# Degrees and gates of a four-layer graph network as products in four column groups of TensorE

## The chip, the cores and the metric

The kernel runs on one core of one Trainium2 chip. A core has TensorE (PE; its weight loads are PEld), VectorE (DVE), ScalarE (ACT), GpSimd (POOL) and SyncE (SP), each with an instruction stream of its own. They meet at semaphores and share the on-chip SBUF and the accumulators in PSUM. The metric is the time of one execution on the device, in microseconds (us), as a median over runs: less is better.

## The reference

Sixteen graphs ("batches") of 1024 nodes with 128 features pass through four layers; each layer is added to its input and layer-normed. The adjacency is 1024 x 1024, of zeros and ones, symmetric. Cut to what matters:

```python
# layer 0: attention with one gate
h = x @ W.T + b;  e = (h @ A) @ h.T;  e = e + e.T
att = softmax(where(adj > 0, e, -9e15), axis=1) * adj
hp = relu(att @ h);  c = sigmoid(concat[x, hp] @ gate_w.T + gate_b)
x = LN(x + c * x + (1 - c) * hp)

# layer 1: thinned adjacency, then three SAGE steps
adj_d = dilate(adj)                       # row after row
def sage(x, Wr, Wx, b):
    deg = clip(sum(adj_d, -1), 1, None)   # the degrees
    out = (adj_d @ x) / deg @ Wr + x @ Wx + b
    return out / norm(out) * mask
# h1, h2, h3: sage, relu and batch norm over all batches, one after the other
x = LN(x + (concat[h1, h2, h3] * mask @ Wl + bl) * mask)

# layer 2: attention with three gates
h, e, att, hp as in layer 0 (masked entries are 0 ahead of the softmax)
i, f, o = [sigmoid(concat[x, hp] @ g_w.T + g_b) for g in ("ig", "fg", "og")]
x = LN(x + o * tanh(sigmoid(i * hp + f * x)))

# layer 3: graph convolution, A = D^-1/2 (adj + I) D^-1/2
h = elu(elu(x @ W0 + b0));  h = elu(A @ (h @ W1) + b1)
x = LN(x + A @ (h @ W2) + b2)
```

## The kernel before

All work of the profile lies in the fast path (from line 640 on). A general fallback behind a run-time flag is compiled in as well and isn't run. A batch's 1024 nodes lie as 8 row tiles (NT) of 128 (P); wide results go in two halves (H2) of 512 columns, a PSUM bank each. Layers 0 and 2 keep features on the partitions for products ("xT", "hT", "hpT", 128 x 1024) and nodes on the partitions for the norms ("xn", "yn").

Stage 1 (lines 882 to 995) does layer 0 batch by batch; the dilation follows (1005 to 1181). Layer 1 (1237 to 1471) goes three times over the batches, as each batch norm needs all of them: first batches 8 to 15, whose thinned adjacency is still in SBUF ("carry", fp8), then 0 to 7, whose adjacency is loaded again ("A8"). In the first of the three steps a batch passes four generators, which take turns: `load`, `first` (of the next batch), `out` (of this one) and `keep` (of the one before). `first` has the degrees (1352 to 1363): `degree_product` multiplies a constant weight of 128 equal columns ("twos", over the tensor "step") with the adjacency, so that every PSUM partition gets the row of the column sums; ACT copies partition 0 as "row" (1357), a DMA turns it to 8 x 128 ("d16"), DVE takes a minimum over it (1360), clips and inverts it (1362, 1363), and a DMA writes it to memory, from where it is read back as "rdeg" on all partitions. Then come the transposes of x, the split of x in "hi" and "lo" (1251 on ACT, 1252 on DVE), the widening of the adjacency to four-byte pieces "a" (1271, 1273) and the product of both (1284), scaled by "rdeg" (1376). `out` multiplies with the two weights (1388), and has the row norms: "o" on DVE (1390), squares on ACT (1396), "ss" on DVE (1397). `keep` transposes the result and makes the product with the adjacency for the next step.

Layers 2 and 3 (1477 to 1660) are one pipeline over the batches. `in_turn` (807) interleaves `after` of batch b-1, `attention` of batch b and `before` of batch b+1. `attention` (1563) runs over 8 row tiles: mask on ACT (1571), scores on PE ("pmm", 723), masked maximum on DVE (1576), exponential on ACT (1580), sums on DVE, and the product with h on PE (1590), accumulated over the tiles in one PSUM tile "acc". `after` (1593) takes the ReLU of it ("hpT", 1596), forms the three gates ("pg", 1600 and 1601), adds the bias (1603), takes the sigmoid through tanh on ACT (1604), combines (1608 to 1614, with the transposes of hpT at 758), norms (741 on DVE, 744 on POOL, 796 on DVE, 798 on ACT) and then does layer 3: A widened to four bytes (1626 on ACT, 1639 on DVE), the transposes, the product with U0 (765), two elus (1498 to 1504), the product with U1 (1513), the propagation (1527), and both again with U2. `before` (1532) applies layer 1's last linear map (765, 1539) and norm, and prepares xT, hT, G and hn.

The order of instructions on each engine isn't the program's order: a scheduler sets it when the kernel is built, from the instructions and what they depend on, so that an edit can move others too. The tiles come from pools with a fixed number of buffers; layer 1's products have four PSUM banks "acc" and four "ph", layers 2 and 3 have two banks "ph".

Layer 0's gate has a helper, `gates` (768 to 780), that the edit uses again. It multiplies a narrow weight (32 columns) with a quarter of the 1024 nodes in each of four column groups of the PE array, side by side, and turns the result to have the nodes on partitions:

```python
for q in range(4):
    nc.tensor.matmul(p[32 * q:32 * q + 32, :], g, x[:, q * N // 4:(q + 1) * N // 4], start=(i == 0),
                     stop=(i == len(pairs) - 1), tile_position=(0, 32 * q))
...
nc.scalar.copy(out, p)
p = psum.tile([P, 2, P], F32, name="pg", tag="h")
for t in range(2):
    nc.tensor.transpose(p[:, t, :], out[:, t * P:(t + 1) * P], identf)
return p.rearrange("p t (q g) -> p q t g", q=4)
```

Of the kernel before, what the change touches and what calls it, by code (L numbers as in the profile page):

```python
# [9 lines left out]
F32 = mybir.dt.float32  # L10
# [12 lines left out]
P = 128  # L23
# [616 lines left out]
def fast_kernel(ctx: ExitStack, tc: tile.TileContext, t: dict, out: bass.AP, flag: bass.AP):  # L640

    nc = tc.nc
    B, N, D = t["x"].shape
    NT = N // P
    H2 = N // 512
# [122 lines left out]
    def gates(psum, out, *pairs):  # L768


        p = psum.tile([P, N // 4], F32, name="pq", tag="h")
        for i, (g, x) in enumerate(pairs):
# [8 lines that stand above are left out]
# [82 lines left out]
    twos = step[:, P:]  # L863
# [18 lines left out]
    with ExitStack() as ph:  # L882

        early = ph.enter_context(tc.tile_pool(name="l0_early", bufs=1, reuse_waits="tile"))
        wts = ph.enter_context(tc.tile_pool(name="l0_w", bufs=1, reuse_waits="tile"))
# [10 lines left out]
        gw = wts.tile([P, 2, 32], F32, name="l0gw")  # L896
# [286 lines left out]
    class Layers23:  # L1183
# [8 lines left out]
        def weights(self, ps_h):  # L1192
            wts = self.wts
            self.Wl = wts.tile([P, 3, P], F32, name="Wl")
            nc.sync.dma_start(self.Wl, nat(t["L1_gnn_Wl"]))
            self.blcol = column(wts, t["L1_gnn_bl"], "blcol")
            self.W2T = transposed(wts, ps_h, matrix(wts, t["L2_gnn_W_w"], "l2W"), "l2WT", "h")
            self.b2 = column(wts, t["L2_gnn_W_b"], "l2b")
            self.As2 = symmetric(wts, ps_h, matrix(wts, t["L2_gnn_A"], "l2A"), "l2As", "h")
            self.gw = wts.tile([P, 2, 3], F32, name="l2gw")  # L1200
            self.gb = wts.tile([P, 3], F32, name="l2gb")
            for i, n in enumerate(("ig", "fg", "og")):
                with nc.allow_non_contiguous_dma(reason="a vector of 256"):
                    nc.sync.dma_start(self.gw[:, :, i], t[f"L2_gnn_{n}_w"].rearrange("o (h d) -> d (o h)", d=P))
                src = t[f"L2_gnn_{n}_b"]
                nc.sync.dma_start(self.gb[:, i:i + 1], bass.AP(tensor=src.tensor, offset=src.offset, ap=[[0, P], [1, 1]]))
            self.U = [matrix(wts, t[f"L3_gnn_W{i}"], f"U{i}") for i in range(3)]
            self.c = [column(wts, t[f"L3_gnn_b{i}"], f"c{i}") for i in range(3)]
            self.nbig = wts.tile([P, 1], F32, name="nbig")
            nc.vector.memset(self.nbig, -BIG)  # L1210
# [26 lines left out]
    with ExitStack() as ph:  # L1237
# [16 lines left out]

        def degree_product(A):

            for h in range(H2):
                c = slice(h * 512, (h + 1) * 512)
                acc = ps_a.tile([P, 512], F32, name="acc")
                for jt in range(NT):  # L1260
                    nc.tensor.matmul(acc, twos[:, :P], A[:, jt, c], start=(jt == 0), stop=(jt == NT - 1))
                yield acc, c

        def widened(A):

# [22 lines left out]
        class Step:  # L1288
# [63 lines left out]
            def first(self, b):  # L1352

                st = self.batches[b]
                row = work.tile([1, N], F16, name="row", bufs=1)
                for acc, c in degree_product(st.A):
                    nc.scalar.copy(row[:, c], acc[0:1, :])
                d16 = small.tile([NT, P], F16, name="d16", bufs=1)
                nc.gpsimd.dma_start(d16, row)
                nc.vector.tensor_reduce(nodeg[:NT, b:b + 1], d16, AX.X, OP.min)  # L1360
                d8 = small.tile([NT, P], F32, name="d8", bufs=1)
                nc.vector.tensor_scalar(d8, d16, 0.5, 1.0, op0=OP.mult, op1=OP.max)
                nc.vector.reciprocal(d8, d8)
                nc.gpsimd.dma_start(rdeg_d[b], d8)
                self.load_rdeg(b)
                yield
                st.hT = work.tile([P, N], F32, name="hT")
                for p, c, _ in turned(ps_h, st.x):
                    nc.scalar.copy(st.hT[:, c], p)
                yield  # L1370
                parts = split(st.x)
                pieces = list(widened(st.A))
                yield
                st.ag = work.tile([P, N], F32, name="ag", bufs=3)
                for acc, c in adjacency_product(pieces, parts):
                    nc.vector.tensor_mul(st.ag[:, c], acc, st.rdeg[:, c])
                    yield
# [99 lines left out]
    with ExitStack() as ph:  # L1477
# [10 lines left out]
        def wide(name, bufs=1, dtype=F32):  # L1488
            return work.tile([P, N], dtype, name=name, bufs=bufs)
# [103 lines left out]
        def after(s, b):  # L1593

            hpT = wide("hpT")
            nc.scalar.activation(hpT, s.acc, AF.Relu)
            pg = ps_h.tile([P, NT, 3], F32, name="pg", tag="h")
            for i in range(NT):
                c = slice(i * P, (i + 1) * P)
                nc.tensor.matmul(pg[:, i, :], s.xT[:, c], gw[:, 0, :], start=True, stop=False)  # L1600
                nc.tensor.matmul(pg[:, i, :], hpT[:, c], gw[:, 1, :], start=False, stop=True)
            gt = small.tile([P, NT, 3], F32, name="gt")
            nc.vector.tensor_add(gt, pg, gb[:, None, :].to_broadcast([P, NT, 3]))
            nc.scalar.activation(gt, gt, AF.Tanh, scale=0.5)
            nc.vector.tensor_scalar(gt, gt, 0.5, 0.5, op0=OP.mult, op1=OP.add)
            yn = rows("yn", 2)
            for p, c, k in turned(ps_h, hpT):
                nc.vector.tensor_mul(yn[:, k, :], tiles3(p), half_rows(gt[:, k, 0]))
            f = rows("x3T")
            nc.vector.tensor_mul(f, s.xn, per_row(gt[:, :, 1]))  # L1610
            nc.vector.tensor_add(yn, yn, f)
            nc.scalar.activation(yn, yn, AF.Tanh, scale=0.5)
            nc.scalar.activation(yn, yn, AF.Tanh, scale=0.5, bias=half)
            nc.vector.tensor_mul(yn, yn, per_row(gt[:, :, 2]))
            nc.vector.tensor_add(s.xn, s.xn, yn)
            yield
            normed(small, s.xn)
            diag = bass.AP(tensor=s.A8.tensor, offset=s.A8.offset, ap=[list(s.A8.ap[0]), [N + P, NT], [1, P]])
            nc.vector.tensor_tensor(diag, diag, identb[:, None, :].to_broadcast([P, NT, P]), op=OP.add, saturate=False)
            dB = wide("dB")  # L1620
            nc.sync.dma_start(dB, bass.AP(tensor=dinv_d.tensor, offset=dinv_d.offset + b * N, ap=[[0, P], [1, N]]))
            yield

            A = work.tile([P, NT, N], F32R, name="A")
            for jt in range(NT // 2):
                nc.scalar.copy(A[:, jt, :], s.A8[:, jt, :])
            db = dinv[:, b * NT:(b + 1) * NT]
            x3T = wide("x3T")
            for p, c, _ in turned(ps_h, s.xn):
                nc.scalar.copy(x3T[:, c], p)  # L1630
            h0 = wide("ehi", 2)
            for p, c in products(ps_h, (U0, x3T)):
                elu(h0[:, c], p, c0)
            h1 = wide("ehi", 2)
            for h in range(H2):
                c = slice(h * 512, (h + 1) * 512)
                elu(h1[:, c], h0[:, c], None)
            for jt in range(NT // 2, NT):
                nc.vector.tensor_copy(A[:, jt, :], s.A8[:, jt, :])
            yield  # L1640
            parts = scaled_parts(h1, U1, db)
            yield
            r = propagated(parts, A, dB)
            h2 = wide("ehi", 2)
            for h in range(H2):
                c = slice(h * 512, (h + 1) * 512)
                elu(h2[:, c], r[:, c], c1)
            yield
            parts = scaled_parts(h2, U2, db)
            yield  # L1650
            r = propagated(parts, A, dB)
            nc.scalar.activation(r, r, AF.Identity, bias=c2)
            yield
            for p, c, k in turned(ps_h, r):
                nc.vector.tensor_add(s.xn[:, k, :], s.xn[:, k, :], tiles3(p))
            normed(small, s.xn)
            nc.gpsimd.dma_start(nat(out[b]), s.xn)
            yield
# [49 lines left out]
```

## Time and profile before

| | |
|---|---|
| time, median of 3 runs | 3050.43 us (3050.39 to 3054.73) |
| span of the profiled execution | 3049.5 us |
| mean granted clock of TensorE | 0.966 |
| layer 1, first step, a batch of the first half | 24.0 us |
| layers 2 and 3, a batch | 70.2 to 72.1 us |

A line of the groups view names the kernel's line, the engine, the operation and its tiles (out<-in), the shape and the count; then the busy time in us and the mean of one in ns; then the engine's idle time just before, and what ended it. A four-byte matmul counts as two instructions, a pass each. A line of the timeline starts with its start and duration in us. In the chain of waits each line is a piece of the work that ended last: start, duration, engine, tile, line, count. In a window, each engine's busy time in the stretch is followed by the number of its instructions, then the granted clock of TensorE (1.00 is full speed), the DMA engines' share and GB/s.

### The profile page before, as it was taken

What the parts mean: (1) busy time and instruction counts of PE and PEld (TensorE: products, weight loads), DVE (VectorE), ACT (ScalarE), POOL (GpSimd) and SP (SyncE); (2) the same over time, 40 slices, a digit from 0 to 9 for tenths busy, and PEclk for the clock granted to TensorE, in tenths of its full rate; (3) what the DMA queues carried; (4) which work ended last, traced back from release to release, by engine and by line L of the source; (5) the groups of instructions that cost most, each with busy time, mean ns of one, the idle gap of its engine ahead of it and who ended that gap; (6) DMA issues with size and microseconds to landing.
All of it is one profiled execution on the core that took longest, in us unless ns stands there. A gap on an engine that the chain in (4) does not pass through costs nothing.

```text
span 3049.5 us, 42855 instructions
## 1 busy us (share of the span) xinstructions
PE 2825.3 (93%) x15187; PEld 1794.2 (59%) x15250; DVE 2325.2 (76%) x5972; ACT 2018.8 (66%) x3425; POOL 315.2 (10%) x292
## 2 busy tenths in 40 slices
PE   7999999996999989999999987999999999999995
PEld 3444444443666657777788873556555555555554
DVE  7898889887999986666678785676766776777665
ACT  5877787773888886655555435666666666666653
POOL 0000000003000001111122231000000000000000
PEclk9999999997999999999999998999999999999997
DMA  5344344430000043223367692011112211111000
GB/s 162 131 159 152 132 138 159 152 118 29 2 2 2 2 158 107 88 91 120 122 231 251 227 336 76 35 63 59 66 57 71 73 57 56 56 56 56 21 14 22
DMA packets 123217, 297.97 MB, mean 98 GB/s; under 512 B 12656, under 2 KB 64624, under 8 KB 115824
## 3 DMA queue, kind: packets, MB, share of 16 engines
q1 hardware_dynamic: 102384, 211.13, 20.6%
q0 software_dynamic: 20608, 84.00, 7.7%
q8 instruction: 122, 2.00, 0.3%
q14 instruction: 103, 0.84, 0.1%
HBM read 211.04 MB, written 84.02 MB: 97 GB/s over the span
## 4 chain that ended last, share of the span: by engine, by line
PE 58%; DVE 21%; ACT 9%; DMA 5%; issue 5%; POOL 3%; SPq 0%; POOLq 0%; ACTq 0%; DVEq 0%
PE acc L1284 9%; PE pmm L723 8%; PE ph L1527 7%; PE acc L1590 6%; PE ph L765 6%; PE ph L758 4%; PE ph L1388 4%; DMA an<-in_adj 3%; ACT xn L798 3%; PE s L1131 2%; PE acc L969 2%; POOL ln_rstd L744 2%; PE ph L1513 2%; DVE mid L1085 2%; DVE ln_st L791 2%
## 5 line engine op out<-in xcount | busy, mean ns | idle before, releaser
L723 PE MATMUL pmm<-G,hT 128*128 128x512 f32 x1024 | 520.2, 630 | 1.9 <-DVE mx L1576 1.4
L723 PEld LDWEIGHTS pmm<-G,hT 128*128 128x128 f32 x1024 | 188.3, 201 | 174.2 <-issue 148.7
L798 ACT ACTIVATE xn<-xn,ln_nb,ln_rstd 128x128 f32<-128x128 f32 x512 | 206.6, 481 | 91.9 <-DVE ln_nb L796 91.9
L1590 PE MATMUL acc<-em,hs 128*128 128x512 f32 x512 | 256.0, 612 | 12.1 <-DVE hs L1587 10.5
L969 PE MATMUL acc<-em,hs 128*128 128x512 f32 x512 | 243.5, 599 | 18.2 <-DVE hs L966 16.8
L1284 PE MATMUL acc<-a,hi 128*128 128x512 f32 x768 | 242.0, 400 | 1.1 <-ACT hi L1251 0.9
L1284 PE MATMUL acc<-a,lo 128*128 128x512 f32 x768 | 241.2, 398 | 1.9 <-DVE lo L1252 1.9
L744 POOL TENSOR_TENSOR ln_rstd<-ln_rstd,mhalf 128x8 f32<-128x8 f32 x64 | 105.4, 1646 | 1324.2 <-DVE ln_rstd L741 1266.2
L1133 ACT ACTIVATE q<-s,negc 128x512 f16<-128x512 f32 x256 | 170.3, 696 | 58.2 <-DVE negc L1112 22.3
L915 ACT ACTIVATE ab<-an 128x1024 bf16<-128x1024 f32 x128 | 134.5, 1052 | 105.8 <-DMA an<-in_adj 66.6
L1131 PE MATMUL s<-step,carry 128*128 128x384 bf16 (+3 forms) x1034 | 197.6, 302 | 7.3 <-DVE carry L1101 3.2
L1576 DVE CUSTOM_DVE_ANT_0 em<-pmm,msk 128x1024 f32<-128x1024 f32 x128 | 156.0, 1219 | 54.7 <-PE pmm L723 51.9
L1145 ACT ACTIVATE carry<-pc,negone 128x512 fp8e4<-128x512 f32 x256 | 166.5, 698 | 35.7 <-PE pc L1144 26.3
L958 DVE CUSTOM_DVE_ANT_0 em<-pmm,msk 128x1024 f32<-128x1024 f32 x128 | 156.1, 1219 | 35.0 <-PE acc L969 30.5
L1571 ACT ACTIVATE msk<-A,nbig 128x1024 bf16<-128x1024 fp8e4 x128 | 146.0, 1141 | 50.2 <-DVE mx L1576 48.4
L1284 PEld LDWEIGHTS acc<-a,lo 128*128 128x128 f32 x768 | 142.9, 188 | 42.8 <-DVE lo L1252 9.5
L918 DVE SCALAR_TENSOR_TENSOR chk<-an 128x1024 fp8e4<-128x1024 f32 x128 | 156.3, 1221 | 14.0 <-DMA an<-in_adj 13.6
L1284 PEld LDWEIGHTS acc<-a,hi 128*128 128x128 f32 x768 | 141.7, 188 | 34.0 <-ACT hi L1251 1.4
L923 DVE TENSOR_SCALAR carry<-pt 128x1024 fp8e4<-128x1024 bf16 x128 | 155.7, 1217 | 6.2 <-PE pt L922 6.1
L969 PEld LDWEIGHTS acc<-em,hs 128*128 128x128 f32 x512 | 90.9, 190 | 113.9 <-issue 87.7
L1388 PE MATMUL ph<-Wx,hT 128*128 128x128 f32 x768 | 152.3, 281 | 4.9 <-DVE l2WT L709 3.2
L962 ACT ACTIVATE em<-em,nmx 128x1024 f32<-128x1024 f32 x128 | 146.9, 1147 | 12.3 <-DVE nmx L960 11.8
(285 smaller groups left out, 6448.6 us busy)
## 6 DMA issues: line engine op xcount, KB each, us to landing
an<-in_adj SPq DMA_DIRECT2D x128, 512.0 KB, 3.9
adj_d<-carry POOLq DMA_DIRECT2D x16, 1024.0 KB, 4.9
A<-dil_d SPq DMA_DIRECT2D x16, 1024.0 KB, 6.6
rdeg<-rdeg_d SPq DMA_DIRECT2D x32, 512.0 KB, 4.2
ag_d<-ag POOLq DMA_DIRECT2D x32, 512.0 KB, 5.5
ag<-ag_d SPq DMA_DIRECT2D x32, 512.0 KB, 6.3
A<-adj_d SPq DMA_DIRECT2D x16, 1024.0 KB, 4.8
xn<-in_x SPq DMA_DIRECT2D x16, 512.0 KB, 4.0
```

What stands on the lines that cost most here:

```text
L723: nc.tensor.matmul(p[:, h * 512:(h + 1) * 512], lhsT, rhs[:, h * 512:(h + 1) * 512], start=True, stop=True)
L744: nc.gpsimd.tensor_tensor(r, r, mhalf[:, :n], op=OP.pow)
L765: nc.tensor.matmul(p, W, x[:, c], start=(i == 0), stop=(i == len(pairs) - 1))
L798: nc.scalar.activation(r[:, i, :], r[:, i, :], AF.Identity, scale=rstd[:, i:i + 1], bias=nb[:, i:i + 1])
L969: nc.tensor.matmul(s.acc[:, c], hs, em[:, c], start=(jt == 0), stop=(jt == NT - 1))
L1131: nc.tensor.matmul(s[:, lo or 0:], y, twos if lo is None else step[:, :512 - lo], start=(j == 0), stop=(j == len(terms) - 1))
L1133: nc.scalar.activation(q[:, h * 512:(h + 1) * 512], s, AF.Abs, bias=st.negc[:, i:i + 1])
L1145: nc.scalar.activation(Y[b][:, hb, ks], pc, AF.Relu, bias=negone, saturate=False)
L1284: nc.tensor.matmul(acc, part[:, jt, :], pieces[h * NT // 2 + i][:, j, :], start=(jt == 0 and p == 0), stop=(jt == NT - 1 and p == 1))
L1388: nc.tensor.matmul(p[:, i * P:(i + 1) * P], x[:, j * P:(j + 1) * P], W, start=(n == 0), stop=(n == 1))
L1527: nc.tensor.matmul(p, part[:, jt, :], A[:, jt, c], start=(jt == 0 and i == 0), stop=(jt == NT - 1 and i == 1))
L1590: nc.tensor.matmul(s.acc[:, c], hs, em[:, c], start=(jt == 0), stop=(jt == NT - 1))
```

## The change

Two products whose results are narrow use one column group of the PE array each in place of the whole. The degrees need a single row of column sums: the weight shrinks from 128 to 32 columns, and the four quarters of the adjacency's columns stream through four column groups side by side. The three gates of layer 2 were products with the activations as weights and 3 columns streaming, two per row tile; now the gate weights, padded from 3 to 32 columns with zeros, are the stationary operand, and the activations stream in four groups, as in layer 0. Both are meant to take less of PE's time. The degrees then come as four pieces of 256 on partitions 0, 32, 64 and 96, in one PSUM bank in place of two, with four copies in place of two. The gates now pass through a copy on ACT and two transposes on PE, with a quarter of the buffer "x3T" as scratch.

```diff
-            self.gw = wts.tile([P, 2, 3], F32, name="l2gw")
+            self.gw = wts.tile([P, 2, 32], F32, name="l2gw")
+            nc.vector.memset(self.gw, 0.0)
...
         def degree_product(A):
 
-            for h in range(H2):
-                c = slice(h * 512, (h + 1) * 512)
-                acc = ps_a.tile([P, 512], F32, name="acc")
-                for jt in range(NT):
-                    nc.tensor.matmul(acc, twos[:, :P], A[:, jt, c], start=(jt == 0), stop=(jt == NT - 1))
-                yield acc, c
+            acc = ps_a.tile([P, 512], F32, name="acc")
+            for jt in range(NT):
+                for q in range(4):
+                    nc.tensor.matmul(acc[32 * q:32 * q + 32, :N // 4], twos[:, :32], A[:, jt, q * N // 4:(q + 1) * N // 4],
+                                     start=(jt == 0), stop=(jt == NT - 1), tile_position=(0, 32 * q))
+            for q in range(4):
+                yield acc[32 * q:32 * q + 1, :N // 4], slice(q * N // 4, (q + 1) * N // 4)
...
                 for acc, c in degree_product(st.A):
-                    nc.scalar.copy(row[:, c], acc[0:1, :])
+                    nc.scalar.copy(row[:, c], acc)
...
             nc.scalar.activation(hpT, s.acc, AF.Relu)
-            pg = ps_h.tile([P, NT, 3], F32, name="pg", tag="h")
-            for i in range(NT):
-                c = slice(i * P, (i + 1) * P)
-                nc.tensor.matmul(pg[:, i, :], s.xT[:, c], gw[:, 0, :], start=True, stop=False)
-                nc.tensor.matmul(pg[:, i, :], hpT[:, c], gw[:, 1, :], start=False, stop=True)
+            pg = gates(ps_h, wide("x3T")[:, :N // 4], (gw[:, 0, :], s.xT), (gw[:, 1, :], hpT))
             gt = small.tile([P, NT, 3], F32, name="gt")
-            nc.vector.tensor_add(gt, pg, gb[:, None, :].to_broadcast([P, NT, 3]))
+            nc.vector.tensor_add(gt.rearrange("p (q t) g -> p q t g", t=2), pg[:, :, :, :3],
+                                 gb[:, None, None, :].to_broadcast([P, 4, 2, 3]))
```

## The prediction

> **What bounds the kernel now.** I read the page first, then groups by line, the chain of waits, the timeline at the changed lines, and windows over whole periods. Part 1 of the page:
>
> ```profile
> PE 2825.3 (93%) x15187; PEld 1794.2 (59%) x15250; DVE 2325.2 (76%) x5972; ACT 2018.8 (66%) x3425; POOL 315.2 (10%) x292
> ```
>
> TensorE is the engine to relieve, but 93% is an average. So I look at each changed place. Layer 1's first step in the chain of waits (start, duration, engine, tile, line):
>
> ```profile
> 1225.44 3.57 PE ph L1388 x32
> 1230.78 8.40 PE acc L1284 x36
> 1240.06 6.77 PE acc L1284 x28
> 1249.43 3.57 PE ph L1388 x32
> ```
>
> The step repeats every 24.0 us and nothing but PE is in it. PE's timeline shows what fills the gap between 1246.83 and 1249.43, and the 0.88 us ahead of 1240.06 (this is the period before and this one):
>
> ```profile
> 1222.68 2.76 PE L1261 MATMUL acc<-carry,step 128*128 128x512 fp8e4 x12
> ...
> 1239.02 1.04 PE L1261 MATMUL acc<-carry,step 128*128 128x512 fp8e4 x4
> ```
>
> These are the degrees: 4 + 12 matmuls of 0.217 us, 3.47 us a batch. The window over one period (duration, then busy time of PE, PEld, DVE, ACT, POOL, the granted clock, DMA share, GB/s) says that PE is full at full clock, with the rest far from it; the second line is a period of the second half, where PE idles 1.57 us:
>
> ```profile
> 1206.78:1230.78 24.00, 24.00 (x129) 18.66 (x129) 16.62 (x28) 14.38 (x19) 3.82 (x6) 1.00 0.27 88
> ...
> 1376.00:1402.00 26.00, 24.43 (x134) 18.92 (x132) 16.75 (x29) 14.69 (x19) 3.83 (x5) 1.00 0.37 123
> ```
>
> Layers 2+3 have a period of 72 us, one batch each. Windows from one gate product to the next:
>
> ```profile
> 2058.60:2130.70 72.10, 70.33 (x267) 42.57 (x265) 50.16 (x155) 47.84 (x94) 5.86 (x4) 0.95 0.18 59
> 2130.70:2200.90 70.20, 68.47 (x265) 41.34 (x264) 49.98 (x155) 47.90 (x94) 5.85 (x4) 0.98 0.17 60
> 2200.90:2272.90 72.00, 70.27 (x266) 42.10 (x265) 50.10 (x155) 48.13 (x94) 5.85 (x4) 0.95 0.18 59
> ```
>
> PE is busy 97% of it, but at a mean clock of 0.95; the period at 0.98 is 1.9 us shorter. One-microsecond windows show where the clock goes, just behind the gates (which run from 2200.93 to 2204.42):
>
> ```profile
> 2203.00:2204.00 1.00, 1.00 (x11) 1.00 (x11) 0.21 (x4) 0.00 (x0) 0.00 (x0) 1.00 0.28 49
> 2204.00:2205.00 1.00, 1.00 (x9) 1.00 (x9) 0.26 (x2) 0.19 (x1) 0.00 (x0) 0.71 0.73 262
> 2205.00:2206.00 1.00, 1.00 (x4) 0.64 (x3) 0.00 (x0) 0.04 (x1) 1.00 (x1) 0.50 0.97 410
> ```
>
> From about 2204.4 to 2207.8 PE runs at half clock: four score matmuls (L723) at 2205.31 take 3.14 us, where two take 0.86 to 1.02 at full clock. Of the 16 batches' gate products nearly all are followed by one such drop, some by two: some 20 stretches of 3.41 us, each costing 1.7 us.
>
> [...]
>
> **The change, part by part.** Layer 0 already runs the gate helper, so most prices stand in groups and in the timeline:
>
> ```profile
> L1601 PE MATMUL pg<-l2gw,hpT 128*128 128x3 f32 x256 | 49.7, 264 | 0.0
> L774 PE MATMUL pq<-hpT,l0gw 128*32 128x256 f32 x128 | 10.8, 391 | 0.0
> L779 PE MATMUL pg<-identf,r 128*128 128x128 f32 x32 | 6.2, 274 | 0.2 <-ACT r L776 0.2
> L776 ACT COPY r<-pq 128x256 f32<-128x256 f32 x16 | 5.8, 360 | 1.9 <-PE pq L774 1.9
> L1357 ACT CAST row<-acc 1x512 f16<-1x512 f32 x32 | 18.3, 572 | 15.8 <-PE acc L1261 15.7
> ```
>
> ```profile
> 84.25 0.64 PE L774 MATMUL pq<-hpT,l0gw 128*32 128x256 f32 x8
> 84.82 1.13 PE L723 MATMUL pmm<-G,hT 128*128 128x512 f32 x2
> ```
>
> *Degrees.* Removed: 16 x 0.217 = 3.47 us. Added: 8 row tiles of 4 groups x 256 columns. A 512-column pass takes 0.217 us, so 256 columns take 0.108, and 8 of them 0.87 us; about 0.1 us for each change of tiling (the layer-0 gates: second four from 84.491 to 84.82, 0.33, against the 0.24 of the first four). The order of the changed program keeps two chunks, now 20 and 12 of 32 matmuls. The first fills PE while it waits for DVE's `lo` (L1252): it shrinks from 0.87 to some 0.6, but `lo` ends when it did, so I count zero. The second is on the path: 2.61 becomes 3 x 0.108 plus 0.1 to 0.25, about 0.55. Saved: 2.05 a period in 8 full periods = 16.5. In the second half (some 5.5 periods of 25.7) PE also waits: DVE's reduction of the row's DMA (L1360) stands ahead of `ss` (L1397), whose end frees the PSUM bank that the next transposes need; the changed order has `ss` first. On the other side the row's four copies (4 x about 0.36 in place of 2 x 0.57 on ACT[...]) make the DMA leave 1.2 us later. Between 0.5 and 2.1; I take 1.0: 5.5. The first batch's product, before the loop, and the switch of halves give 4. Sum 26 (15 to 35).
>
> *Gates on PE.* Removed: 32 passes from 2200.93 to 2204.42, 3.49 us. Added: 16 passes of 256 columns in groups of four, twice the 0.57 of the second operand in the timeline = 1.1, and two transposes, 0.2 to 0.3. Saved 2.2 a batch, 35 over 16. If the clock then stays up, 20 x 1.7 = 34 more, 2.1 a batch.
>
> *Gates' new waits.* Before, DVE's add took `pg` 0.18 us after PE's last gate. Now ACT's copy stands between, and two transposes behind it. In the changed order that copy is queued behind two 1.04-us casts of A (L1626 before), so the gates reach DVE some 1 us later than PE has finished; half a score product fills PE meanwhile. The bigger move: the tanh of the gates stood ahead of the eight norms (L798, 8 x 0.4 = 3.2 us) on ACT, and now stands behind them, and those wait for POOL's power (1.64 us). Behind that tanh wait DVE's gate arithmetic, `yn`, and PE's next batch input (L765). Followed through row durations: L765 at 10.0 us after the gates' start instead of 9.5; the transposes of `xn` 25.7 instead of 25.1; the product with U1 (L1513) at 39.0 instead of 37.7, with PE idle some 3.7 us ahead of it, as elu's halves and the diagonal add stand in front on DVE; the first propagation (L1527) at 44.5 instead of 43.0. That period ends at about 72, so nothing is won. My walk is good to about 2 us a period.
>
> But the changed order alternates between two patterns from batch to batch, and the other (elu's halves interleaved on DVE and ACT, U-products in two parts) is nearer to before's. For it I take the full PE gain, 2.2 + 2.1 = 4.3. Eight periods at 0 and eight at 4.3: 34; I round to 32. The memset of the gate weights is once, beside other weight loads: zero. The strided add reads the same 24 values: zero.
>
> Sum: 26 + 32 = 58; 3050.4 - 58 = 2992.
>
> **The rivals.** (A) *PE bounds everywhere and the clock stays up.* For it: 97% busy in the period, ACT at 48 and DVE at 50 of 72, and the short 70.20 period. Against: the walked waits. 26 + 69 + 2 at the tail (no filler there) = 97: 2953. (B) *The gates' gain is eaten by the new waits in both patterns, only layer 1 gains*: the tanh behind the norms delays every later step of the batch. 3050 - 26 = 3024. (C) *Slower:* layers 2+3 get longer by 2.3 us a period[...] (in before, the waits near the `xn` transposes bring a drop in about half of the periods), 16 x 2.3 = 37 against 26: 3061. Speaking against it: DVE and ACT have over 20 us free in each period, and the walk stays near 72 even with a wait of 3.7.
>
> **How the numbers follow.** My forecast 0.48, A 0.21, B 0.19, C 0.12. The likeliest gives 2992. The range leaves out C and the far end of A: 2945 (A with 8 more from layer 1) to 3042 (B with layer 1 at 15 and 7 lost in layers 2+3). Faster by over 0.2% (below 3044): 0.48 + 0.21 + most of B = 0.86; same 0.04; slower 0.10.
>
> **What would show it.** In layer 1 a period of 21.9 in place of 24.0, with PE still full and its degree chunks at about 0.6 and 0.55; in the second half about 24.7. In layers 2+3 gates of 1.1 us, no 0.50 window directly behind them; alternating periods of about 68 and 72. A is right if both patterns lie at 68, B if both lie at 72. Wrong would be: an `lo` or ACT bound in layer 1 (period stays near 23), or PE idle over 5 us a period ahead of U1 in both patterns, with clock drops there.

## The result and the profile after

The median falls from 3050.41 us to 3017.41 us (four runs each, 3015.01 to 3019.96 after): a ratio of 0.989, 95% interval 0.987 to 0.991. That is 33 us of the 58 that were forecast. The changed kernel's line numbers are one above those of the kernel before from 1201 on (1252 is now 1253) and two above from 1265 to the gates (1388 is now 1390, 1513 is 1515); the degrees stay at 1261, and behind the gates the numbers are one below (the tanh, 1604, is 1603).

The page's busy times after:

```profile
PE 2743.8 (91%) x15219; PEld 1723.1 (57%) x15282; DVE 2328.2 (77%) x5973; ACT 2027.8 (67%) x3473; POOL 324.3 (11%) x292
```

TensorE is busy 81 us less, and the time falls by 33: the rest came back as waits. Groups of the changed operations after:

```profile
L774 PE MATMUL pq<-hpT,l2gw 128*32 128x256 f32 x128 | 9.9, 380 | 0.0
L779 PE MATMUL pg<-identf,x3T 128*128 128x128 f32 x32 | 6.8, 295 | 1.3 <-ACT x3T L776 1.3
L776 ACT COPY x3T<-pq 128x256 f32<-128x256 f32 x16 | 5.8, 365 | 1.2 <-PE pq L774 1.2
L1359 ACT CAST row<-acc 1x256 f16<-1x256 f32 x64 | 23.2, 363 | 1.4 <-PE acc L1261 0.9
```

The L1261 matmuls in PE's timeline, and two periods of layer 1's first step as windows (first half, second half; columns as in the prediction):

```profile
1245.50 0.51 PE L1261 MATMUL acc<-carry,step 128*32 128x256 fp8e4 x12
1259.88 0.73 PE L1261 MATMUL acc<-carry,step 128*32 128x256 fp8e4 x20
```

```profile
1223.90:1245.90 22.00, 21.81 (x148) 17.83 (x144) 16.33 (x28) 14.66 (x21) 4.31 (x5) 1.00 0.28 96
1380.40:1404.70 24.30, 21.90 (x148) 17.93 (x144) 16.35 (x28) 14.78 (x21) 4.31 (x5) 1.00 0.38 131
```

The first half runs at 22.0 us with PE still full but for 0.2. In the second half PE now idles 2.4 us of a period of 24.3, where it idled 1.57 of a window of 26. Three periods of layers 2 and 3:

```profile
2042.80:2113.70 70.90, 65.74 (x253) 37.81 (x252) 50.64 (x156) 48.35 (x95) 6.83 (x4) 0.98 0.17 60
2113.70:2184.80 71.10, 67.40 (x253) 38.98 (x252) 50.14 (x155) 48.23 (x95) 5.85 (x4) 0.98 0.16 60
2184.80:2255.90 71.10, 65.89 (x249) 37.73 (x248) 50.57 (x155) 48.16 (x95) 6.82 (x4) 0.98 0.17 60
```

PE's work fell from about 70 to between 65.7 and 67.4 us, the period only from 72 to 71. Over 12 steady batches, from gates to gates, the means say it closer: PE busy 70.0 us before and 66.7 after, idle 1.75 and 4.2, the period 71.7 and 70.8. One-microsecond windows show the clock shortly behind the gates (which start at 2184.82 and leave PE free at 2185.82), and later in the same batch:

```profile
2187.00:2188.00 1.00, 1.00 (x8) 0.67 (x6) 1.00 (x2) 0.00 (x0) 0.00 (x0) 1.00 0.66 90
2188.00:2189.00 1.00, 1.00 (x4) 0.49 (x3) 0.35 (x5) 0.84 (x1) 0.65 (x1) 1.00 0.77 311
...
2215.00:2216.00 1.00, 1.00 (x5) 0.78 (x4) 0.47 (x5) 1.00 (x2) 0.50 (x1) 0.50 0.00 0
2216.00:2217.00 1.00, 1.00 (x2) 0.33 (x1) 1.00 (x1) 1.00 (x4) 0.00 (x0) 0.50 0.00 0
```

Behind the gates the clock stays at 1.00 in all 16 batches; before, 14 of 16 had a stretch of 0.50 there. But one stretch a batch is left, in most batches 26 to 36 us after the gates. From the first gates to the last, the stretches of 3.41 us at half clock fell from 27 to 15. PE's two longest waits in this batch (start, duration, what ran, and the idle time before it with its releaser):

```profile
2211.89 1.87 PE L758 MATMUL ph<-identf,xn 128*128 128x128 f32 x5 [2.19 <-ACT xn L798]
2222.76 2.22 PE L1515 MATMUL ph<-U,ehi 128*128 128x128 f32 x16 [1.63 <-DVE ehi L1502]
```

The stretch in this batch begins at 2214.5, 2.6 us after the end of the first wait; behind the second there is none. Of the 15 stretches, 11 begin within 3 us of the end of a wait of 1.9 to 2.6 us (three of them 0.3 to 0.4 us ahead of that end), but four have only a wait of 0.5 us ahead of them, and behind the waits of 1.5 to 1.6 us ahead of U1 there is none. So waits and stretches go together without the one being shown to set the other.

By stages, from starts in the two timelines (but for rounding, the parts add up to the two spans):

| stage | before | after | change |
|---|---|---|---|
| to the first degree matmul (layer 0, dilation) | 1145.1 | 1145.2 | 0.1 |
| to the first product with the weights (L1388) | 16.3 | 21.0 | +4.7 |
| first period of the step | 15.9 | 13.1 | -2.8 |
| 8 periods of the first half | 192.0 | 176.8 | -15.2 |
| 5 periods of the second half | 128.6 | 122.9 | -5.7 |
| to layer 2's first ReLU (L1596) | 420.6 | 426.0 | +5.4 |
| first to last ReLU, 15 batches of layers 2 and 3 | 1042.6 | 1027.4 | -15.2 |
| end | 88.5 | 84.8 | -3.7 |

The sixth row is not shown to be the change: three experiments below with the changed degrees (deg_only, lo_first, tanh_copy) took 419 to 424. Nor is the first row steady: over the experiments it lay between 1139 and 1151. The stages between are steady to about a microsecond, so the readings below go by stages, and by totals only where they are large.

### The profile page after: what moved, and what is told of

Same layout as the page of the kernel before. It is cut to its first block, busy times and chain, and to the rows that moved or that the text cites. A ratio compares the mean times of both kernels' runs of the same rounds, so it can differ in the third digit from the quotient of the medians.

```text
span 3017.3 us, 42970 instructions
## 1 busy us (share of the span) xinstructions
PE 2743.8 (91%) x15219; PEld 1723.1 (57%) x15282; DVE 2328.2 (77%) x5973; ACT 2027.8 (67%) x3473; POOL 324.3 (11%) x292
## 4 chain that ended last, share of the span: by engine, by line
PE 38%; DVE 22%; issue 21%; ACT 9%; DMA 6%; POOL 5%; POOLq 0%; SPq 0%; DVEq 0%; ACTq 0%
PE ph L1529 8%; PE acc L1286 7%; PE ph L765 5%; DMA an<-in_adj 4%; PE acc L1592 4%; PE pmm L723 3%; PE ph L1390 3%; POOL ln_rstd L744 3%; ACT xn L798 3%; DVE ln_st L791 3%; PE ph L758 3%; DVE em L1578 2%; PE ph L1515 2%; PE acc L969 2%; ACT em L962 2%
## 5 line engine op out<-in xcount | busy, mean ns | idle before, releaser
L723 PE MATMUL pmm<-G,hT 128*128 128x512 f32 x1024 | 505.6, 611 | 6.7 <-DVE mx L1578 6.7
L723 PEld LDWEIGHTS pmm<-G,hT 128*128 128x128 f32 x1024 | 179.0, 193 | 174.2 <-issue 139.8
L744 POOL TENSOR_TENSOR ln_rstd<-ln_rstd,mhalf 128x8 f32<-128x8 f32 x64 | 112.2, 1753 | 1333.4 <-DVE nmx L1580 607.0
L1133 ACT ACTIVATE q<-s,negc 128x512 f16<-128x512 f32 x256 | 170.5, 697 | 58.0 <-DVE negc L1112 22.3
```

The costliest lines, as they stand in the source:

```text
L723: nc.tensor.matmul(p[:, h * 512:(h + 1) * 512], lhsT, rhs[:, h * 512:(h + 1) * 512], start=True, stop=True)
L744: nc.gpsimd.tensor_tensor(r, r, mhalf[:, :n], op=OP.pow)
L1133: nc.scalar.activation(q[:, h * 512:(h + 1) * 512], s, AF.Abs, bias=st.negc[:, i:i + 1])
```

## The experiments

**The two parts alone.** In the first the gates are as before, in the second the degrees.

```diff
# deg_only: the diff of degree_product and of the copy alone
+                    nc.tensor.matmul(acc[32 * q:32 * q + 32, :N // 4], twos[:, :32], A[:, jt, q * N // 4:(q + 1) * N // 4],
...
# gates_only: the diff of gw, pg and gt alone
+            pg = gates(ps_h, wide("x3T")[:, :N // 4], (gw[:, 0, :], s.xT), (gw[:, 1, :], hpT))
```

> The degrees in column groups alone, gates as before. Theory (the two parts add up, since the order on each engine is the changed kernel's in layer 1 and the old kernel's in layers 2 and 3): layer 1's first step with periods of 22.0 and 24.3 us, layers 2 and 3 at 72 us, total 3050 - 14 = 3036. Rival (the parts depend on each other[...]): total off that sum by more than 5 us.

> The gates in column groups alone, degrees as before. Theory (additive): layer 1 at 24.0 and 25.7 us as before, layers 2 and 3 at 70.3 to 71.1 us a batch, total 3050 - 18 = 3032. Rival: total off that by more than 5 us.

Measured: 3028.87 us (ratio 0.993, 0.991 to 0.994) and 3033.75 us (0.994, 0.993 to 0.996). The gates alone are as expected. The degrees alone are 7 us better than expected in total, but not in their stages: periods of 22.0 and 24.3, and 71.94 us a batch in layers 2 and 3; 5.7 us of the total come from the stretch ahead of the first degree matmul, where nothing differs. So the parts add up by stages.

**Is it the place of the tanh?** In the changed kernel's layers 2 and 3 ACT's timeline has this order behind the copy of the gates:

```profile
2186.35 0.37 ACT L776 COPY x3T<-pq 128x256 f32<-128x256 f32 x1
2188.16 1.15 ACT L1573 ACTIVATE msk<-A,nbig 128x1024 bf16<-128x1024 fp8e4 x1 [1.44 <-DVE mx L1578]
...
2190.23 3.19 ACT L798 ACTIVATE xn<-xn,ln_nb,ln_rstd 128x128 f32<-128x128 f32 x8 [0.83 <-DVE ln_nb L796]
2193.32 0.21 ACT L1603 ACTIVATE gt<-gt 128x24 f32<-128x24 f32 x1
```

The gates' sum is there at 2188.3 (DVE, L1601); its tanh runs 5 us later, behind the eight norms. In the kernel before it ran ahead of them:

```profile
2204.81 0.22 ACT L1604 ACTIVATE gt<-gt 128x24 f32<-128x24 f32 x1 [2.16 <-DVE gt L1603]
...
2209.67 3.17 ACT L798 ACTIVATE xn<-xn,ln_nb,ln_rstd 128x128 f32<-128x128 f32 x8
```

In tanh_copy the tanh takes the place of the copy (in layer 2; layer 0's gate keeps its copy):

```diff
-        nc.scalar.copy(out, p)
+            nc.scalar.activation(out, p, AF.Tanh, scale=0.5, bias=bias)
...
-            nc.vector.tensor_add(gt.rearrange("p (q t) g -> p q t g", t=2), pg[:, :, :, :3],
-                                 gb[:, None, None, :].to_broadcast([P, 4, 2, 3]))
-            nc.scalar.activation(gt, gt, AF.Tanh, scale=0.5)
-            nc.vector.tensor_scalar(gt, gt, 0.5, 0.5, op0=OP.mult, op1=OP.add)
+            nc.vector.tensor_scalar(gt.rearrange("p (q t) g -> p q t g", t=2), pg[:, :, :, :3], 0.5, 0.5, op0=OP.mult, op1=OP.add)
```

> Both parts, but the gates' tanh is put in the place of the plain copy out of PSUM (the bias as a column), so that it stands ahead of the eight norms on ACT and DVE's add falls away; PE's work is the same. Theory W (the gain of PE in layers 2 and 3 went into waits behind the late tanh): period 68 to 69 us in place of 70.8, PE idle 2 us a period less, total about 3017 - 30 = 2987. Rival P (the waits belong to the rest of the batch's chain, elu and norms, and the tanh's place is not what sets them): period stays at 70 to 71, total 3010 to 3018.

Measured: 2990.18 us (0.980, 0.979 to 0.982). A window over a period:

```profile
2170.80:2240.00 69.20, 64.62 (x252) 37.18 (x250) 50.40 (x155) 48.38 (x94) 5.85 (x4) 1.00 0.17 61
```

Nearly every period is 69.2, the order repeats from batch to batch, and the clock is 1.00 in all the steady periods. But PE is not less idle, as theory W had it: it idles 4.6 us a batch (4.2 in the changed kernel), in pieces of at most 1.6 us, ahead of scores, attention products and the product that takes `yn`. What went is the stretch at half clock, and the 1.6 us a batch that the period is shorter are about what it took (1.7). So the total fits W, but by way of the clock, not of less idle time. To part the tanh's place from the dropped instructions, tanh_late keeps tanh_copy's instructions and queues that tanh behind the final norms of the batch before:

```diff
+            with tc.issue_after(behind[-1]):
+                nc.scalar.activation(out, p, AF.Tanh, scale=0.5, bias=bias)
...
-            normed(small, s.xn)
+            done.append(normed(small, s.xn))
```

> As tanh_copy, the same instructions, but the gates' tanh is issued behind the eight final norms of the batch before on ACT, where the changed kernel has its own tanh. Theory W (its place behind the norms costs the waits): period in layers 2 and 3 up from 69.2 to 70.8 us or more, PE's wait ahead of the product with U1 is back with a clock drop behind it, total about 2990 + 16 x 1.8 = 3018. Rival P (what helped in tanh_copy was the dropped add of DVE and the shorter chain, not the place): period below 69.8, total below 3000.

Measured: 3055.78 us (1.002, 1.001 to 1.003), periods of 72.8 and 73.9 us in turn: 65 us more than tanh_copy, with the same instructions. It is worse than the expected 3018, since here the transposes stand behind the late tanh too. Two of PE's waits (from one window of the timeline):

```profile
2147.25 2.08 PE L1525 MATMUL ph<-U,ehi 128*128 128x128 f32 x8 [3.43 <-DVE ehi L1512]
...
2195.23 2.84 PE L765 MATMUL ph<-hb,Wl 128*128 128x512 f32 x6 [1.28 <-DVE yn L1614]
```

The wait ahead of U1 (here L1525) is back, and stretches at half clock with it (one or two a batch): over two periods PE is busy 67.1 us a batch in place of 64.6, and idle 6.3 in place of 4.6. So it is the tanh's place among the norms, and what the scheduler arranges around it, that costs. P falls. The changed kernel's own small tanh was not moved by itself, so its share alone isn't shown.

**Is PE still the bound?** tanh_double is tanh_copy with the gate products run twice, so that the gates' sums come out doubled:

```diff
-            pg = gates(ps_h, wide("x3T")[:, :N // 4], (gw[:, 0, :], s.xT), (gw[:, 1, :], hpT), bias=gb)
+            pg = gates(ps_h, wide("x3T")[:, :N // 4], *((gw[:, 0, :], s.xT), (gw[:, 1, :], hpT)) * 2, bias=gb)
```

> As tanh_copy, with both operands of the gate products run twice, 1.1 us more of PE's time a batch (the sums come out doubled, so the gates' values are not the reference's). Theory (with PE idle 4.6 us of 69.2 a batch, PE no longer sets the period; waits for DVE and ACT do): period 69.2 to 69.7. Rival (PE's order is the bound, any pass added is paid in full): period 70.3.

Measured: 2988.2 us (two runs), periods of 69.1:

```profile
2093.90:2163.00 69.10, 65.58 (x267) 37.45 (x267) 50.55 (x153) 47.90 (x93) 5.85 (x4) 1.00 0.18 61
```

PE works 1 us more and the period is no longer. So at this place PE is not the bound, and by this a further cut of its time at the gates would bring nothing; PE's other work in the period was not varied.

**Where the half clock comes from.** pad64 is the kernel before with wider gate weights:

```diff
-            self.gw = wts.tile([P, 2, 3], F32, name="l2gw")
+            self.gw = wts.tile([P, 2, 64], F32, name="l2gw")
+            nc.vector.memset(self.gw, 0.0)
...
-            pg = ps_h.tile([P, NT, 3], F32, name="pg", tag="h")
+            pg = ps_h.tile([P, NT, 64], F32, name="pg", tag="h")
```

> The kernel before with the gate weights padded from 3 to 64 columns: the same 32 passes, paced by the same weight loads, but 64 columns stream in each (the pads' results are not read). Theory K[...]: gates still take 3.5 us, and no stretch at 0.50 directly behind them; layers 2 and 3 gain up to 1.7 us a batch, unless the order, which the padding also shifts, gives it back. Rival (it comes from the wait or the weight loads themselves): stretches at 0.50 stay within 5 us of the gates in most batches.

Measured: 3067.48 us (1.006, 1.004 to 1.008), so slower, but the clock is what was asked. The windows at the end of a gate block (to 2437.6) and behind it:

```profile
2437.00:2438.00 1.00, 1.00 (x11) 0.97 (x10) 0.18 (x1) 0.00 (x0) 0.00 (x0) 1.00 0.59 162
2438.00:2439.00 1.00, 1.00 (x8) 0.72 (x7) 0.73 (x3) 0.98 (x3) 0.00 (x0) 1.00 1.01 306
2439.00:2440.00 1.00, 1.00 (x4) 0.52 (x3) 1.00 (x3) 1.00 (x4) 0.00 (x0) 1.00 0.03 5
```

With 64 columns none of the 16 blocks (3.3 to 3.6 us each; in eight batches the first row tile's first pair ran some 11 us ahead of the rest, from which the block is counted) has a half clock in it or in the 4 us behind it; with 3 columns 14 of 16 had. PE was as busy by the profile in both, 1.00. So what theory K expected of the clock came: the stretches at half clock went with the 3 columns, though the order around the blocks moved as well. The time went the other way: 72.9 us a batch, with waits of up to 3 us in another order, and stretches at half clock after waits of 2 to 3 us.

**The start of layer 1.** In the changed kernel's timeline of the first batch, DVE and PE:

```profile
1153.98 0.27 DVE L1362 TENSOR_REDUCE nodeg<-d 8x1 f32<-8x128 f16 x1 [7.61 <-DMA d<-row]
1155.30 1.15 DVE L1253 TENSOR_TENSOR lo<-n,hi 128x1024 fp32r<-128x1024 f32 x1
```

```profile
1156.50 1.22 PE L1286 MATMUL acc<-a,lo 128*128 128x512 f32 x2 [4.70 <-DVE lo L1253]
```

`lo` stands behind the reduction that waits for the row's round trip by DMA. In the kernel before it stood ahead:

```profile
1150.27 1.22 DVE L1252 TENSOR_TENSOR lo<-n,hi 128x1024 fp32r<-128x1024 f32 x1 [3.91 <-ACT hi L1251]
...
1153.44 0.27 DVE L1360 TENSOR_REDUCE nodeg<-d 8x1 f32<-8x128 f16 x1 [1.94 <-DMA d<-row]
```

lo_first puts it ahead again, in that batch alone:

```diff
+                if b == order[0]:
+                    with tc.issue_after(self_lo[-1].ins):
+                        self.degree(b, d16)
```

> Both parts, but in the first batch of layer 1 DVE's subtraction that gives lo is issued ahead of the reduction that waits for the row's DMA; all other instructions keep their order. Theory (lo queued behind that reduction cost the start 4.8 us): PE's wait of 4.7 us at about 1152 goes, the first product with the weights starts near 1161.4 in place of 1166.2, total 3017 - 4.7 = 3012.7. Rival (the degrees' round trip through memory sets the start): first product with the weights stays at 1166, total 3017.

Measured: 3011.4 us (0.987, 0.986 to 0.989); from the first degree matmul to the first product with the weights 17.0 us in place of 21.0. The theory holds.

**The second half.** The timeline of the changed kernel (SP's and POOL's DMA issues, DVE, PE):

```profile
1358.28 0.32 SPq L1333 DMA_DIRECT2D A<-dil_d  x1
1358.58 0.51 POOL L1361 DMA_DIRECT2D d<-row  x1 [7.60 <-ACT row L1359]
...
1363.31 0.28 DVE L1362 TENSOR_REDUCE nodeg<-d 8x1 f32<-8x128 f16 x1 [2.47 <-DMA d<-row]
1365.65 0.65 DVE L1399 TENSOR_REDUCE ss<-ph 128x4 f32<-128x512 f32 x1
...
1371.52 0.73 PE L1261 MATMUL acc<-A,step 128*32 128x256 fp8e4 x20 [1.41 <-DVE ag L1425]
1373.26 0.73 PE L1286 MATMUL acc<-a,lo 128*128 128x512 f32 x2 [1.00 <-DVE lo L1253]
```

The row's 2 KB leave 0.3 us behind the 1 MB of the next adjacency and are used 4.7 us after; the second half of `ss`, and with it `rn`, `n` and `lo`, come late. The kernel before had this wait too:

```profile
1395.06 0.32 SPq L1331 DMA_DIRECT2D A<-dil_d  x1
1396.03 0.51 POOL L1359 DMA_DIRECT2D d<-row  x1 [8.28 <-ACT row L1357]
...
1400.04 0.27 DVE L1360 TENSOR_REDUCE nodeg<-d 8x1 f32<-8x128 f16 x1 [2.39 <-DMA d<-row]
```

There the row left 1.0 us behind the load and was used 4.0 us after; counted from the load's issue, the reduction began 5.0 us later in both kernels. So a mend here wins back an old wait as well. Two experiments take this apart: a8_late puts the load later (beyond the lines below, the whole `load` of the first step is moved behind `first`), one_copy the row earlier.

```diff
# a8_late
+                            with tc.issue_after(rdeg_ins[-1]):
+                                nc.sync.dma_start(st.A.bitcast(F32), dil8_d[b])
...
# one_copy
-                row = work.tile([1, N], F16, name="row", bufs=1)
-                for acc, c in degree_product(st.A):
-                    nc.scalar.copy(row[:, c], acc)
+                row = work.tile([P, N // 4], F16, name="row", bufs=1)
+                acc = degree_product(st.A)
+                nc.scalar.copy(row, acc[:, :N // 4])
...
-                nc.gpsimd.dma_start(d16, row)
+                nc.gpsimd.dma_start(d16, row[0:P:32, :])
```

> The changed kernel with its four row copies, but the 1 MB load of the adjacency in the second half is issued on SP behind the load of rdeg, and so well behind the row's DMA. Theory L (the row's DMA lands late because it leaves 0.3 us behind that load; the reduction waits for it on DVE, ahead of ss): the row lands some 2 us after its issue in place of 4.7, PE's waits of 1.4 and 1.0 us go, second half 22.0 a batch in place of 24.3. Rival Q (the four copies themselves hold up ACT): second half stays above 23.5.

> The changed kernel with one ACT copy of 128 x 256 for the degrees in place of four of 1 x 256, nothing else. Theory L and Q both: second half 22.0 a batch as in lo_tanh_one, since the row's DMA leaves ahead of the load; the first batch's start some 1 to 2 us earlier than 21.0 after its first degree matmul. If the second half stays at 24.3, the gain in lo_tanh_one came from another of its mends.

Measured: 3003.1 us (0.986, 0.983 to 0.989) and 3005.34 us (0.986, 0.984 to 0.989). A period of the second half of each, a8_late first:

```profile
1350.50:1372.20 21.70, 21.70 (x145) 18.04 (x145) 16.41 (x28) 14.83 (x21) 4.31 (x5) 1.00 0.35 129
```

```profile
1385.40:1407.40 22.00, 21.81 (x148) 17.83 (x144) 16.44 (x28) 13.58 (x18) 4.64 (x5) 1.00 0.41 145
```

With the four copies kept and only the load put later, PE is full and the period is 21.7: theory L, and Q falls, as ACT works as long as before (14.83 us). With one copy the row leaves first by itself, and is used 1.9 us after its issue:

```profile
1386.76 0.84 POOL L1360 DMA_DIRECT2D d<-row  x1 [6.00 <-ACT row L1358]
1387.58 0.32 SPq L1332 DMA_DIRECT2D A<-dil_d  x1
1388.67 0.27 DVE L1361 TENSOR_REDUCE nodeg<-d 8x1 f32<-8x128 f16 x1 [0.48 <-DMA d<-row]
```

One expectation was missed: the single copy did not shorten the start (21.8 us there). Its row left 0.9 us earlier, 3.8 us after the first degree matmul in place of 4.7, but an adjacency load stands ahead of it there too (issued 3.8 us before it), and the reduction began 8.8 us after that load in both kernels, with `lo` behind it. In a8_late, which has no load there, the start took 18.1 us.

**All mends together.** lo_tanh_one is the changed kernel with the edits of lo_first, tanh_copy and one_copy.

> Both parts with three mends: lo ahead in the first batch, the tanh in place of the copy, and the degrees' four rows copied in one ACT copy of 128 x 256, from which the DMA takes partitions 0, 32, 64 and 96. Theory (stages add up; the single copy frees 1.1 us of ACT and lets the DMA leave 1.1 us earlier, which is on no path in the first half): first half at 22.0, second half 24.3 to 23.5, layers 2 and 3 at 69.2, total 2990 - 4 - 3 = 2983. Rival (the row's DMA sets the second half's period): second half 23.2 or less a batch, total 2977. Rival (neither): 2986.

Measured: 2971.7 us (0.975, 0.973 to 0.977), the best of all. The start takes 14.9 us, the periods of the first step behind it are 22.0 to 22.3, layers 2 and 3 run at 69.2. It beats the expectation by 11 us: the second half went below the 23.2 of the rival, whose total was 2977.

## Why the prediction was right or wrong

The range held the time and the direction was right, but 25 us of the expected gain are missing, and it ended nearer to rival B (3024) than to the forecast (2992). The range was 97 us wide and held both, so that the number fell into it says little of the mechanism; the stages say more.

*Degrees, first half: right.* 2.05 us a period expected, 15.2 / 8 = 1.9 measured; the chunk on the path is 0.51 us (0.55 expected), the hidden one still ends with `lo`.

*Degrees, second half: right size, wrong way.* 1.0 expected, 5.7 / 5 = 1.1 measured (four periods 1.4 to 1.6 shorter, one 0.2 longer; why that one is left open). "The changed order has `ss` first" holds for one half of `ss` only; the reduction stands ahead of the other half and still waits. That the row's DMA leaves late was seen, but not what makes it land late, before the change and after it: the adjacency load ahead of it. Without that collision the second half gains 2.3 us more a batch (one_copy). The copies out of PSUM took what was expected, 4 x 0.363 us in place of 2 x 0.572. But what they cost here came through a DMA, not through ACT: with the four copies kept and the load put later, ACT works as long and the period is 21.7 (a8_late).

*Degrees, start: wrong.* The step that failed is "The first batch's product, before the loop, and the switch of halves give 4". The faster product let the scheduler put `lo` behind a wait for a DMA: 4.7 us lost at the start against 2.8 won in the first period. I had compared the order in steady periods only. With the rows of the table up to the second half, layer 1 gave 19.0 of 26.

*Gates on PE: right.* 3.49 us before, 1.00 and two transposes after (1.1 expected).

*Clock: right cause, 20 of 34 us.* The half clock went with the 3-column passes: 14 of 16 gate blocks have it with 3 columns, none with 64 (pad64). What in those passes brings it was not shown. With them the 20 stretches behind the gates that the forecast counted went. But 7 more stood elsewhere in the batches, and after the change there are 15: 12 stretches fewer at 1.7 us each.

*New waits: seen, and undervalued.* Of the 4.3 us a batch that PE was to gain in all, 3.3 came (70.0 to 66.7), but its waits grew by 2.4 (1.75 to 4.2), so that 0.9 was left of the 2.0 expected (32 over 16). The tanh behind the norms was named as the bigger move, and tanh_late shows that its place is worth tens of us. The failed step is "Eight periods at 0 and eight at 4.3": I took the second pattern for near to before's from DVE's and PE's order, but ACT's has the tanh behind the norms in both. From gates to gates the periods measured lie at 70.3 to 71.1, not at 68 and 72; the waits ahead of U1 are 1.5 to 2.6 us, not 3.7. Layers 2 and 3 gave 15.2 + 3.7 = 18.9 us of 32.

*Rivals.* A would have needed PE as the bound of layers 2 and 3. It isn't at the gates: with the period mended to 69.2, a microsecond of PE more costs nothing (tanh_double). C came within reach: tanh_late is that case, with the same work on PE. That waits bring the half clock is not shown, though: before the change 13 batches have the same wait of 0.63 to 0.64 us ahead of the transposes of `xn`, and in 7 of them a stretch begins 2.0 to 2.8 us behind it.

## What to carry to other kernels

When an edit shortens one engine's work under a scheduler, read the new order on every engine, at the first batch and in each phase, and look for what now stands behind a long group or a DMA wait: here the edit brought 33 us, and mending three such places another 46, in part from a wait that the kernel before had as well. Narrow results packed side by side come out as more, smaller pieces; take them out of PSUM in one instruction over all partitions, with the next function in it (the tanh, the cast), before they enter a queue: here one copy of 128 x 256 took 0.36 us (one_copy), each of the four of 1 x 256 as much (0.363). And where a small transfer that others wait for stands behind a large one, try it ahead: here that took 2.3 us off a period.

## What the runs showed of the hardware

Two blocks of 32 passes that the profile shows alike differ in the clock that goes with them. PE is busy throughout in both (3.49 us in the kernel before, 3.3 to 3.6 us in pad64), and so are its weight loads (3.49 us of those 3.49; 1.00 and 0.97 of pad64's microseconds from 2436.0 and 2437.0). With 3 columns streaming 14 of 16 have a stretch at half clock at their end or within 2 us of it, with 64 columns none. The busy share of PE, 1.00 in both, doesn't tell the two apart; the edit between them is the number of columns, and the order around the blocks moved with it.

In column groups 32 fp8 matmuls of 256 columns took 0.99 us at the first batch, from 1145.17 to the next instruction at 1146.16, where 16 of 512 columns took 3.45, from 1145.07 to 1148.52: 3.5 times faster. The four matmuls of a row tile start within 0.01 us, and four follow four after 0.109 us; but from the last four to the next instruction, on the whole array, it is 0.21 us. So the 0.99 us have some 0.1 us for that change in them; without it, in the kernel before, the instruction behind the last degree matmul came after 0.215 us, at the pace of the matmuls ahead (0.216).

A row of 2 KB was used 1.9 us after its issue when it left 0.8 us ahead of a 1 MB load (one_copy). In the steady periods of the first half, with no adjacency load close ahead, it was used 1.5 us (the kernel before) and 2.2 us (the changed one) after its issue. Behind the load the time went by the load's issue and not by the row's own: in the second half the reduction that waits for the row began 4.9 to 5.2 us after the load's issue, whether the row left 1.0 us behind it (the kernel before) or 0.3 us (the changed one).

Neither the total of PE's idle time nor the mere presence of waits told the clock: 4.6 us idle a batch in pieces of at most 1.6 us went with 1.00 throughout (tanh_copy), while 4.2 us with waits of up to 2.6 us went with one stretch at half clock a batch (the changed kernel).
